# Odd taps of S through ScalarE and GpSimd, and the order of a turn's side work, in a chain of modulated 1-D convolutions

## Chip, core and metric

The kernel runs on one core of one Trainium2 chip. The metric is device time in microseconds of one execution; the kernel before takes 475.72 us (median of three runs, 475.56 to 475.97). Engines are named as in the profile: PE is TensorE's matmul, PEld its weight load, DVE is VectorE, ACT is ScalarE, POOL is GpSimd, SP is SyncE, which issues nearly all DMAs.

## The reference

x is (128, 64, 1024), the style (128, 128). Four layers of a convolution of 3 taps, 64 to 64 channels, whose weights are scaled per sample by the style and normalised, follow each other without a nonlinearity; the second doubles the length and blurs, the fourth blurs and halves it. The result is added to x.

```python
def _layer(x, style, w, b, mw, mb, typ):
    s = style @ mw.T + mb
    weight = SCALE * w * s[:, None, :, None]
    demod = lax.rsqrt(jnp.sum(weight * weight, axis=(2, 3)) + EPS)
    weight = weight * demod[:, :, None, None]
    if typ == 'same':
        out = jax.vmap(_conv_same)(x, weight) + b[None, :, None]
    elif typ == 'upsample':
        out = jax.vmap(_conv_up)(x, weight.transpose(0, 2, 1, 3)) + b[None, :, None]
        out = _blur(out, 2.0 * blur_k, (1, 1))
    elif typ == 'downsample':
        xb = _blur(x, blur_k, (2, 2))
        out = jax.vmap(_conv_down)(xb, weight) + b[None, :, None]
    return out
...
out = x
for i, typ in enumerate(('same', 'upsample', 'same', 'downsample')):
    out = _layer(out, style, weights[i], biases[i], mod_w[i], mod_b[i], typ)
x = x + out
```

## The kernel before

All four layers are linear, so the kernel first multiplies their weights together: for each sample one convolution of 9 taps with 64 x 64 weights (Wf), and this is applied to x. The first and last three columns of each row, where padding matters, are computed on their own ("ends"), in pieces spread over the run.

Work is grouped in 32 groups q of four samples. Matmuls use the array as four quarters of 64 x 64, so one group's four samples go through it together; each fp32 matmul leaves two records in the trace. The stages of a group, with the tiles that they write:

- scale3 (ACT): wd, the scaled taps of the last layer. For q of 3 and more the tile holds five blocks: three taps and two sums of neighbours (w3x).
- stage1 (PE, ACT): psS is the product of wd with the weights of the layer before, S its five scaled taps. For q of 0, 1, 2 and 6 this is done directly by stage1. For the others stage1_a and stage1_b use a scheme with seven products instead of nine: stage1_a forms four of the blocks from five products, copied with the factor tBn (the negative of tB); stage1_b adds two more products into PSUM, from which two taps come by a VectorE instruction per half (L481: sum times tB minus a block), and GpSimd adds two blocks for one tap (L484).
- stage2 (PE, ACT): psR is S times the blurred up-sampling taps E, R its seven scaled taps. From group 8 to 30 sums of S are shared: share_sums (DVE) writes two more slots of S, share (PE) multiplies them into an unused stretch of the bank of psA, share_copy (ACT) copies the result into psR as seeds, and stage2_rest adds the rest.
- stage3_b, stage3_a (PE, ACT): psA and psW, then Wf. r_sums (POOL) makes two sums of R for the last products of stage3_b; four ACT copies seed psW for stage3_a.
- combine_a, combine_b (DVE): H, three sums of taps for a convolution with five products where nine would be needed.
- in_g01, in_g2 (DVE), in1, in2 (POOL), in3, in04 (DVE): the matching sums G and T of three planes of x. X is loaded plane by plane into two buffers.
- conv3, conv1, conv2 accumulate in psA, conv4 in Y, conv0 in psA; copy_m3 (ACT), sum1 and sum2 (DVE) take the partial results out in between; outputs (ACT) writes the three output planes o, stored by SP.

The order on each engine is the order of the program text. A turn of the main loop (turn_of(q), groups 4 to 28) works on several groups at once: the convolution of q and of n = q + 1, stage 2 and 3 of c = q + 2, stage 1 of s = q + 4. On PE a turn reads: stage2_rest, conv2, stage3_b, conv4, stage3_a, conv3, stage1_a, conv0, stage1_b, share, conv1. The first four groups go through early_turn, which has the same pieces in another order: there S of group q + 3 is used by stage 2 at the start of the next turn, while in turn_of it is used two turns later. psS, psR and psW share one pair of PSUM banks. SIDE, TABLES and LATE are tables of small pieces (scale tables, ends) by turn: side(SIDE, q) runs VectorE pieces of up to a few instructions.

Of the kernel before, what the change touches and what calls it, by code (L numbers as in the profile page):

```python
# [54 lines left out]
C = 64  # L55
K = 3
# [7 lines left out]
def kernel(  # L64
# [381 lines left out]
    def stage1(q, pool=None, engs=(nc_a, nc_a), between=None):  # L446

        wd = chain[q]
        ps = unit(pool or ps_w, f"psS{q}")
        for k, (at, at1) in enumerate(((0, 3), (3, 1), (1, 4))):  # L450
            tap_matmul(ps, wd, at, 2, woi[2][:, k, :], EVEN, first=k == 0)
            tap_matmul(ps, wd, at1, 1, woi[2][:, k, :], slice(1, 2), last=k == K - 1)
        if between:
            between()
        st, _ = s_tiles(q)
        for r in range(2):
            scaled_copy(engs[r], flat(st[r][:, 1:6]), ps[r][:, : 5 * C], tB[:, q, r : r + 1])
        chain[q] = st
        return ps

    def stage1_a(q, ps=None):

        ps = ps or unit(ps_w, f"psS{q}")
        wd = chain[q]
        tap_matmul(ps, wd, 2, 2, w2n[:, 0, :], EVEN, first=True)
        tap_matmul(ps, wd, 3, 2, w2n[:, 2, :], EVEN)
        tap_matmul(ps, wd, 1, 1, w2n[:, 1, :], slice(1, 2))
        st, t = s_tiles(q)
        for r in range(2):
            scaled_copy(nc_a, flat(st[r][:, :4]), ps[r][:, C : 5 * C], tBn[:, q, r : r + 1])  # L470
        chain[q] = wd, ps, st, t

    def stage1_b(q):

        wd, ps, st, t = chain[q]
        tap_matmul(ps, wd, 2, 1, w2n[:, 3, :], slice(3, 4))
        tap_matmul(ps, wd, 4, 1, w2n[:, 4, :], slice(4, 5), last=True)
        for r in range(2):
            p1 = st[r][:, 0:1, :].to_broadcast([P, 2, C])
            sums = ps[r][:, 2 * C : 6 * C].rearrange("c (a b o) -> c a b o", a=2, b=2)[:, :, 0]  # L480
            nc_v.scalar_tensor_tensor(  # L481
                st[r][:, 4:6, :], sums, tB[:, q, r : r + 1], p1, op0=ALU.mult, op1=ALU.subtract
            )
        nc_g.tensor_add(t[:, :, 2], t[:, :, 2], t[:, :, 0])  # L484
        chain[q] = st
        whole[q] = t

# [10 lines left out]

    def share_sums(q):
        t = whole[q]  # L500
        nc_v.tensor_add(t[:, :, 6:8], t[:, :, 1:5:3], t[:, :, 2:6:3])

    def chain_matmul(dst, weight, st, slots, last=False):
        for r, rows in enumerate(HALF):
# [10 lines left out]
    def share(q, ps):  # L515

        at = [NB + 4 + i * C for i in range(3)]
        p12, p34 = ([b[:, i:j] for b in ps] for i, j in zip(at, at[1:]))
        chain_matmul(p12, E[:, 2], chain[q], slice(6, 7))
        chain_matmul(p34, E[:, 6], chain[q], slice(6, 7))  # L520
        chain_matmul(p34, E[:, 5], chain[q], slice(7, 8), True)
        shared_ps[q] = [b[:, at[0] : at[2]] for b in ps]

    def share_copy(q):
# [10 lines left out]
    def stage2_rest(q):  # L535

        ps = shared_ps.pop(q)
        block = lambda i, n=1: [b[:, i * C : (i + n) * C] for b in ps]
        apart = [b[:, : 4 * C].rearrange("c (a b o) -> c a b o", a=2, b=2)[:, :, 0] for b in ps]
        plan = (  # L540
            (apart, E[:, 0], slice(1, 4, 2)),
            (block(1), Ed[:, 0], slice(2, 3)),
            (block(2), Ed[:, 1], slice(1, 2)),
            (block(3), E[:, 2], slice(3, 4)),
            (block(3), Ed[:, 2], slice(2, 3)),
            (block(4), Ed[:, 3], slice(1, 2)),
            (block(4), E[:, 4], slice(3, 4)),
            (block(5, 2), E[:, 8], slice(2, 4)),
            (block(5), E[:, 6], slice(3, 4)),
            (block(1, 2), E[:, 1], slice(4, 6)),  # L550
            (block(2), E[:, 3], slice(4, 5)),
            (block(3), Ed[:, 4], slice(5, 6)),
            (block(4), Ed[:, 5], slice(4, 5)),
            (block(5), E[:, 7], slice(5, 6)),
        )
# [21 lines left out]
    def stage2_taps(q, taps, ps):  # L577

        st = chain[q]
        for n in taps:  # L580
            e = n - 2
            if e % 2 == 0:
                a, lo, m = slice(1, 4), e // 2 + 1, 3
            else:
                a, lo, m = slice(4, 6), (e + 3) // 2, 2
# [1136 lines left out]
```

## Time and profile before

| | us |
|---|---|
| median of three runs | 475.72 |
| span of the profiled execution | 475.5 |
| PE, convolutions on psA (L803, T with H) busy | 185.9 |
| PE, convolutions on psA and Y (L803, T with Wf) busy | 63.7 + 62.4 |
| PE, stage 2 with sharing (L506, psR) busy | 46.8 |
| DVE, G in two pieces (L712) busy | 49.0 + 27.7 |
| DVE, odd taps of S (L481) busy, 56 instructions | 16.7 |
| ACT, S from psS in stage1_a (L399) busy, 56 instructions | 23.5 |
| POOL, addition in S (L484) busy, 28 instructions | 21.6 |

For the profiled execution there is no time but its span; the three runs beside it were timed by themselves. In a profile row of the order of time the first number is the start in us from the span's start, the second the length, then engine, line, operation, the tiles as out<-in, and the count; in brackets stands idle time of the engine just before, with what ended it. "issue" is a stop for which the trace shows no semaphore. The granted TensorE clock is 0.998 of full speed on average. DMA moves 149 GB/s on average: 70.71 MB, nearly all on queue q1.

### The profile page before, as it was taken

The page shows a single profiled execution, that of the slowest core. Times are in us where ns is not written, and L with a number is a line of the kernel's source. Part 1 is how long each engine was busy: PE and PEld are TensorE (multiplying, and loading weights), DVE is VectorE, ACT ScalarE, POOL GpSimd, SP SyncE. Part 2 cuts the span into 40 slices and gives each one's busy share as a digit, 9 for nine tenths or more (in the row PEclk, how much of TensorE's full clock was granted, in tenths as well). Part 3 has the DMA queues.
Part 4 walks back from the last instruction along what each step waited for, and adds up shares of the span by engine and source line. Part 5 has one row for each costly group of instructions (what it writes and reads, how often), then busy time and mean ns, then how long its engine had stood idle before and what let it go on. Part 6 is the DMA issues. An engine that isn't in the chain of part 4 may idle for free.

```text
span 475.5 us, 26771 instructions
## 1 busy us (share of the span) xinstructions
PE 469.7 (99%) x11932; PEld 349.5 (74%) x11932; DVE 417.3 (88%) x694; ACT 312.0 (66%) x711; POOL 165.8 (35%) x200
## 2 busy tenths in 40 slices
PE   9999999999999999999999999999999999999996
PEld 6987788777678876677776677766788787876653
DVE  3889998879989998899979899979998999999896
ACT  4565657577766676766667666667666777766464
POOL 3634033664444342233432233422333423243200
PEclk9999999999999999999999999999999999999999
DMA  5237456535445554345544454543555544455225
GB/s 176 71 115 224 150 151 180 152 113 177 139 145 166 166 166 136 123 150 169 163 150 126 130 168 152 178 124 121 152 164 169 164 145 147 148 152 161 80 91 193
DMA packets 52707, 70.71 MB, mean 149 GB/s; under 512 B 6000, under 2 KB 50672, under 8 KB 52592
## 3 DMA queue, kind: packets, MB, share of 16 engines
q1 hardware_dynamic: 52368, 68.78, 46.3%
q8 instruction: 93, 1.52, 1.4%
q10 hardware_dynamic: 224, 0.22, 0.1%
q14 instruction: 22, 0.18, 0.1%
HBM read 35.36 MB, written 33.62 MB: 145 GB/s over the span
## 4 chain that ended last, share of the span: by engine, by line
PE 99%; DVE 0%; ACT 0%; issue 0%
PE psA L803 47%; PE Y L803 12%; PE psR L506 9%; PE psW L621 7%; PE psA L621 7%; PE psS L428 6%; PE psR L589 5%; PE psA L506 2%; PE Y L1044 2%; PE Y L183 1%; PE Y L379 1%; PE psM L220 0%; PE psE L1044 0%; PE Y L255 0%; DVE o L882 0%; PE psM L255 0%
## 5 line engine op out<-in xcount | busy, mean ns | idle before, releaser
L803 PE MATMUL psA<-T,H 64*64 64x340 f32 x2304 | 185.9, 446 | 0.0
L803 PEld LDWEIGHTS psA<-T,H 64*64 64x64 f32 x2304 | 90.7, 133 | 46.9 <-issue 2.5
L712 DVE SCALAR_TENSOR_TENSOR G<-X 128x1376 f32<-128x1376 f32 (+2 forms) x65 | 78.0, 1206 | 0.2
L776 POOL TENSOR_TENSOR T<-G 128x684 f32<-128x684 f32 x28 | 46.3, 1652 | 73.7 <-DVE G L712 73.7
L484 POOL TENSOR_TENSOR S<-S 128x128 f32<-128x128 f32 x28 | 21.6, 772 | 139.7 <-ACT S L399 139.6
L399 ACT ACTIVATE R<-psR,tC 128x448 f32<-128x448 f32 x63 | 36.6, 631 | 43.6 <-PE psR L506 25.8
L803 PE MATMUL psA<-T,Wf 64*64 64x340 f32 x768 | 63.7, 446 | 0.0
L803 PE MATMUL Y<-T,Wf 64*64 64x340 f32 x768 | 62.4, 451 | 0.0
L712 DVE SCALAR_TENSOR_TENSOR Y<-m,psA 128x340 f32<-128x340 f32 x62 | 32.0, 516 | 28.2 <-PE psA L803 26.9
L399 ACT ACTIVATE psW<-psA 128x128 f32<-128x128 f32 x100 | 19.3, 268 | 49.1 <-PE psA L621 45.0
L790 DVE TENSOR_TENSOR T<-G 128x1368 f32<-128x1368 f32 (+1 forms) x33 | 50.8, 1541 | 0.0
L399 ACT ACTIVATE Wf<-psW,t 128x256 f32<-128x256 f32 (+2 forms) x76 | 32.7, 480 | 26.7 <-PE psW L621 26.4
L761 DVE TENSOR_TENSOR T<-X 128x684 f32<-128x684 f32 x32 | 47.7, 1492 | 0.0
L506 PE MATMUL psR<-S,E 64*64 64x64 f32 (+1 forms) x1472 | 46.8, 237 | 0.0
L781 POOL TENSOR_TENSOR T<-G 128x684 f32<-128x684 f32 x28 | 46.5, 1660 | 0.0
L428 PEld LDWEIGHTS psS<-wd,w2n 64*64 64x64 f32 x1120 | 35.1, 133 | 12.9 <-issue 0.3
L506 PEld LDWEIGHTS psR<-S,E 64*64 64x64 f32 x1472 | 39.5, 134 | 4.9 <-ACT psR L529 0.2
L803 PEld LDWEIGHTS Y<-T,Wf 64*64 64x64 f32 x768 | 30.3, 132 | 16.8
L803 PEld LDWEIGHTS psA<-T,Wf 64*64 64x64 f32 x768 | 29.8, 133 | 14.5
L880 ACT ACTIVATE o<-psA,tb,td 128x340 f32<-128x340 f32 x63 | 37.1, 648 | 5.0 <-PE psA L803 2.8
L880 ACT ACTIVATE o<-y,tb,td 128x340 f32<-128x340 f32 x62 | 38.5, 678 | 0.0
L880 ACT ACTIVATE o<-Y,tb,td 128x340 f32<-128x340 f32 x62 | 36.1, 639 | 2.8 <-PE Y L803 2.0
(180 smaller groups left out, 840.4 us busy)
## 6 DMA issues: line engine op xcount, KB each, us to landing
out<-o SPq DMA_DIRECT2D x191, 170.0 KB, 2.6
X<-in_x SPq DMA_DIRECT2D x150, 172.0 KB, 3.4
X<-in_x SPq DMA_DIRECT2D x14, 516.0 KB, 5.0
par<-in_params SPq DMA_DIRECT2D x3, 192.0 KB, 3.8
Xe<-in_x_ends SPq DMA_DIRECT2D x1, 512.0 KB, 4.5
out<-Oe SPq DMA_DIRECT2D x2, 96.0 KB, 2.1
out<-o ACTq DMA_DIRECT2D x1, 170.0 KB, 2.8
par<-in_params SPq DMA_DIRECT2D x1, 160.0 KB, 2.7
```

Source lines behind the costliest of these rows:

```text
L399: nc_a.activation(dst, src, AF.Copy, scale=f)
L428: nc.tensor.matmul(ps[r][cols, at * C : (at + n) * C], weight[rows], wd[c if r == 0 else 1 - c][rows, taps], start=first, stop=last, skip_ ...
L506: nc.tensor.matmul(dst[r][cols], weight[rows], st[c if r == 0 else 1 - c][rows, slots, :], start=False, stop=last, skip_group_check=True,)
L589: nc.tensor.matmul(ps[r][cols, lo * C : (lo + m) * C], E[rows, e + 2, :], src[rows, a, :], start=(n == 0), stop=(n == 8), skip_group_check ...
L621: nc.tensor.matmul(dst[r][cols], weight[rows], t[rows, c, slots, :], start=first, stop=last, skip_group_check=True,)
L712: nc_v.scalar_tensor_tensor(out, x, f, y, op0=ALU.mult, op1=op)
L761: nc_v.tensor_sub(t[:, pairs, 0, :NJ], plane(X, 3, pairs), plane(X, 1, pairs))
L776: eng.tensor_add(t[:, :, 0, :NJ], plane(g, 2), plane(g, 1))
L781: eng.tensor_sub(t[:, :, 1, :NJ], plane(g, 2), plane(g, 1))
L790: nc_v.tensor_sub(t[:, pairs, :, :NJ], both(a, PL), both(b, 1))
L803: nc.tensor.matmul(ps[s][cols, :NB], w, Ts[q, tag][rows, c, i, g : g + NB], start=(g == 0 and (m == 3 or alone)), stop=(g == K - 1), skip_ ...
L880: nc_a.activation(dst, src, AF.Identity, bias=add, scale=d3)
```

## The change

S's five taps take slots 0 to 4 in their own order (before: 1, 4, 2, 5, 3), and all readers follow. stage1 multiplies each tap in one matmul of three blocks instead of one of two and one of one. stage1_a copies its four blocks into slots 0, 2, 4 and 6, and GpSimd's addition comes there. stage1_b copies the two odd sums by ScalarE into slots 1 and 3, and GpSimd subtracts the block in slot 6 from both; VectorE's instruction is gone. In turn_of, scale3(s) stands behind stage2's copies of R instead of at the end of the turn before; share and share_copy stand ahead of outputs(q, 1); in_g01 follows in_g2; the side pieces stand at the end of the turn before theirs, behind in3 and in1.

```diff
-        for k, (at, at1) in enumerate(((0, 3), (3, 1), (1, 4))):
-            tap_matmul(ps, wd, at, 2, woi[2][:, k, :], EVEN, first=k == 0)
-            tap_matmul(ps, wd, at1, 1, woi[2][:, k, :], slice(1, 2), last=k == K - 1)
+        for k in range(K):
+            tap_matmul(ps, wd, k, K, woi[2][:, k, :], slice(0, K), first=k == 0, last=k == K - 1)
...
-            scaled_copy(engs[r], flat(st[r][:, 1:6]), ps[r][:, : 5 * C], tB[:, q, r : r + 1])
+            scaled_copy(engs[r], flat(st[r][:, :5]), ps[r][:, : 5 * C], tB[:, q, r : r + 1])
...
     def stage1_a(q, ps=None):
-        tap_matmul(ps, wd, 2, 2, w2n[:, 0, :], EVEN, first=True)
-        tap_matmul(ps, wd, 3, 2, w2n[:, 2, :], EVEN)
-        tap_matmul(ps, wd, 1, 1, w2n[:, 1, :], slice(1, 2))
+        tap_matmul(ps, wd, 1, 2, w2n[:, 0, :], EVEN, first=True)
+        tap_matmul(ps, wd, 2, 2, w2n[:, 2, :], EVEN)
+        tap_matmul(ps, wd, 4, 1, w2n[:, 1, :], slice(1, 2))
         st, t = s_tiles(q)
         for r in range(2):
-            scaled_copy(nc_a, flat(st[r][:, :4]), ps[r][:, C : 5 * C], tBn[:, q, r : r + 1])
+            src = ps[r][:, C : 5 * C].rearrange("c (a o) -> c a o", o=C)
+            scaled_copy(nc_a, st[r][:, 0:7:2, :], src, tBn[:, q, r : r + 1])
+        nc_g.tensor_add(t[:, :, 2], t[:, :, 2], t[:, :, 6])
...
     def stage1_b(q):
-        tap_matmul(ps, wd, 2, 1, w2n[:, 3, :], slice(3, 4))
-        tap_matmul(ps, wd, 4, 1, w2n[:, 4, :], slice(4, 5), last=True)
+        tap_matmul(ps, wd, 1, 1, w2n[:, 3, :], slice(3, 4))
+        tap_matmul(ps, wd, 3, 1, w2n[:, 4, :], slice(4, 5), last=True)
         for r in range(2):
-            p1 = st[r][:, 0:1, :].to_broadcast([P, 2, C])
-            sums = ps[r][:, 2 * C : 6 * C].rearrange("c (a b o) -> c a b o", a=2, b=2)[:, :, 0]
-            nc_v.scalar_tensor_tensor(
-                st[r][:, 4:6, :], sums, tB[:, q, r : r + 1], p1, op0=ALU.mult, op1=ALU.subtract
-            )
-        nc_g.tensor_add(t[:, :, 2], t[:, :, 2], t[:, :, 0])
+            src = ps[r][:, C : 5 * C].rearrange("c (a b o) -> c a b o", a=2, b=2)[:, :, 0]
+            scaled_copy(nc_a, st[r][:, 1:4:2, :], src, tB[:, q, r : r + 1])
+        nc_g.tensor_sub(
+            t[:, :, 1:4:2], t[:, :, 1:4:2], t[:, :, 6:7].to_broadcast([P, 2, 2, C])
+        )
...
     def turn_of(q):
         stage2(c)
+        if s < NQ and not entry:
+            scale3(s)
...
         in_g2(c)
-        side(SIDE, q)
+        in_g01(c)
+        if entry:
+            side(SIDE, q)
+        conv0(q, *((2,) if entry else range(K)))
+        if entry:
+            conv1(n, 0, 1)
+        if s < NQ:
+            stage1_b(s)
         if q in SMALL:
             l, bs = SMALL[q]
             nc_v.memset(high(bs.stop - bs.start), 0.0)
-        conv0(q, *((2,) if entry else range(K)))
-        if entry:
-            conv1(n, 0, 1)
-        outputs(q, 1)
-        if s < NQ:
-            stage1_b(s)
-        in_g01(c)
         if sharing(q):
             share(c + 1, banks(q))
             share_copy(c + 1)
+        outputs(q, 1)
         outputs(q, 0)
...
         in1(c, nc_g)
-        if s + 1 < NQ:
-            scale3(s + 1)
+        side(SIDE, q + 1)
```

The readers of S (share_sums, share, stage2_rest, stage2_taps) change slot numbers only. Three places show what moves.

ScalarE in a turn of the main loop, from the copy m (of psA) on; y and psA are the sources of two output planes, psR the seeds, R the taps of stage 2, wd those of scale3. Before:

```order
L842 COPY m_13_3994<-psA_3884 128x680
L880 ACTIVATE o_3972<-y_12_3792,tb,td 128x340 x2
L529 COPY psR_0_4042<-psA_3614 128x256
L529 COPY psR_1_4043<-psA_3614 128x256
L880 ACTIVATE o_3972<-psA_3614,tb,td 128x340 x2
L399 ACTIVATE wd_0_4068<-w3x,tA 128x320
L399 ACTIVATE wd_1_4070<-w3x,tA 128x320
L399 ACTIVATE R_4128<-psR_0_4042,tC 128x448
L399 ACTIVATE R_4128<-psR_1_4043,tC 128x448
```

The same stretch of the change:

```order
L842 COPY m_13_3960<-psA_3849 128x680
L399 ACTIVATE S_3956<-psS_0_3942,tB 128x2x64
L399 ACTIVATE S_3956<-psS_1_3943,tB 128x2x64
L529 COPY psR_0_4003<-psA_3578 128x256
L529 COPY psR_1_4004<-psA_3578 128x256
L880 ACTIVATE o_3937<-y_12_3756,tb,td 128x340 x2
L880 ACTIVATE o_3937<-psA_3578,tb,td 128x340 x2
L399 ACTIVATE R_4091<-psR_0_4003,tC 128x448
L399 ACTIVATE R_4091<-psR_1_4004,tC 128x448
L399 ACTIVATE wd_0_4094<-w3x,tA 128x320
L399 ACTIVATE wd_1_4096<-w3x,tA 128x320
```

Two copies out of psS come in ahead of the seeds, the y outputs go behind the seeds, and the wd copies behind R.

VectorE in the same turn, from in04 (L790) to the step on Y of sum2; G is written by in_g2 (342 columns twice) and in_g01 (688 twice), L501 is share_sums, L761 in3, Ye and g side work. Before:

```order
L790 TENSOR_TENSOR T_13_3996<-G_3729 128x4x342
L501 TENSOR_TENSOR S_3721<-S_3721 128x2x128
L712 SCALAR_TENSOR_TENSOR G_3999<-X_105 128x2x342
L1066 TENSOR_TENSOR Ye_161<-Ye_161,c_156 128x64x6
L481 SCALAR_TENSOR_TENSOR S_3991<-psS_0_3977,tB,S_3991 128x128
L481 SCALAR_TENSOR_TENSOR S_3991<-psS_1_3978,tB,S_3991 128x128
L712 SCALAR_TENSOR_TENSOR G_3999<-X_105 128x2x688
L712 SCALAR_TENSOR_TENSOR y_13_4062<-psA_3884,m_13_3994 128x680
L761 TENSOR_TENSOR T_14_4064<-X_105 128x2x342
L712 SCALAR_TENSOR_TENSOR Y<-m_13_3994,psA_3884 128x340 x2
```

The same stretch of the change:

```order
L790 TENSOR_TENSOR T_13_3962<-G_3694 128x4x342
L501 TENSOR_TENSOR S_3685<-S_3685 128x2x128
L712 SCALAR_TENSOR_TENSOR G_3965<-X_105 128x2x342
L712 SCALAR_TENSOR_TENSOR G_3965<-X_105 128x2x688
L712 SCALAR_TENSOR_TENSOR y_13_4027<-psA_3849,m_13_3960 128x680
L761 TENSOR_TENSOR T_14_4029<-X_105 128x2x342
L1016 SCALAR_TENSOR_TENSOR g_159<-par,g_159 128x192 x2
L712 SCALAR_TENSOR_TENSOR Y<-m_13_3960,psA_3849 128x340 x2
```

The two instructions on S are gone, the two pieces of G follow each other, and the side work (now that of the next turn) stands right ahead of the step on Y.

TensorE in stage1 of group 1, one tap before (psS is the result, wd the moving operand):

```order
L428 MATMUL psS_371<-wd_0_309,par 64x128
L428 MATMUL psS_371<-wd_1_311,par 64x128 x2
L428 MATMUL psS_371<-wd_0_309,par 64x128
L428 MATMUL psS_371<-wd_0_309,par 64x64
L428 MATMUL psS_371<-wd_1_311,par 64x64 x2
L428 MATMUL psS_371<-wd_0_309,par 64x64
```

and of the change all three taps:

```order
L428 MATMUL psS_359<-wd_0_297,par 64x192
L428 MATMUL psS_359<-wd_1_299,par 64x192 x2
L428 MATMUL psS_359<-wd_0_297,par 64x192 x2
L428 MATMUL psS_359<-wd_1_299,par 64x192 x2
L428 MATMUL psS_359<-wd_0_297,par 64x192 x2
L428 MATMUL psS_359<-wd_1_299,par 64x192 x2
L428 MATMUL psS_359<-wd_0_297,par 64x192
```

Eight matmuls of a tap become four, twelve fewer for each of the four groups that stage1 serves.

More of the change, by code (lines that the diff above doesn't have):

```diff
@@ L518, in share @@
         p12, p34 = ([b[:, i:j] for b in ps] for i, j in zip(at, at[1:]))
-        chain_matmul(p12, E[:, 2], chain[q], slice(6, 7))
-        chain_matmul(p34, E[:, 6], chain[q], slice(6, 7))
-        chain_matmul(p34, E[:, 5], chain[q], slice(7, 8), True)
+        chain_matmul(p12, E[:, 2], chain[q], slice(5, 6))
+        chain_matmul(p34, E[:, 6], chain[q], slice(5, 6))
+        chain_matmul(p34, E[:, 5], chain[q], slice(6, 7), True)
         shared_ps[q] = [b[:, at[0] : at[2]] for b in ps]
@@ L540, in stage2_rest @@
         plan = (
-            (apart, E[:, 0], slice(1, 4, 2)),
+            (apart, E[:, 0], slice(0, 5, 4)),
             (block(1), Ed[:, 0], slice(2, 3)),
-            (block(2), Ed[:, 1], slice(1, 2)),
-            (block(3), E[:, 2], slice(3, 4)),
+            (block(2), Ed[:, 1], slice(0, 1)),
+            (block(3), E[:, 2], slice(4, 5)),
             (block(3), Ed[:, 2], slice(2, 3)),
[L546 to L554, printed above, removed]
+            (block(4), Ed[:, 3], slice(0, 1)),
+            (block(4), E[:, 4], slice(4, 5)),
+            (block(5, 2), E[:, 8], slice(2, 5, 2)),
+            (block(5), E[:, 6], slice(4, 5)),
+            (block(1, 2), E[:, 1], slice(1, 4, 2)),
+            (block(2), E[:, 3], slice(1, 2)),
+            (block(3), Ed[:, 4], slice(3, 4)),
+            (block(4), Ed[:, 5], slice(1, 2)),
+            (block(5), E[:, 7], slice(3, 4)),
         )
```

6 lines of the change are left out of this document (3 added, 3 removed).

## The prediction

> **What bounds the kernel now.** I read the page first: shares by engine, the chain of work that ended last, and the DMA queues.
>
> ```profile
> PE 469.7 (99%) x11932; PEld 349.5 (74%) x11932; DVE 417.3 (88%) x694; ACT 312.0 (66%) x711; POOL 165.8 (35%) x200
> ...
> PE 99%; DVE 0%; ACT 0%; issue 0%
> ...
> q8 instruction: 93, 1.52, 1.4%
> ```
>
> TensorE carries 99% of the chain. VectorE is 88% busy but never on it, so work taken from VectorE shortens nothing by itself; only time in which TensorE issues no matmul can be won. Busy time hides such gaps, since matmul ends are modelled and bridge them. So I next measured whole turns of the main loop, from one copy of m to the next, in the view of busy time by stretches (length, then the busy time of PE, PEld, DVE, ACT, POOL):
>
> ```profile
> 140.73:154.73 14.00, 14.00 (x392) 11.33 (x388) 12.79 (x21) 9.79 (x25) 6.25 (x6) 1.00 0.50 154
> 225.87:239.71 13.84, 13.84 (x392) 9.84 (x388) 13.51 (x23) 9.86 (x25) 4.98 (x4) 1.00 0.49 157
> 342.68:356.86 14.18, 13.98 (x391) 11.26 (x387) 13.21 (x20) 9.85 (x24) 4.82 (x4) 1.00 0.49 151
> 398.47:412.40 13.93, 13.93 (x391) 11.26 (x387) 12.94 (x20) 9.87 (x25) 4.81 (x4) 1.00 0.50 154
> ```
>
> All four do the same matmuls. The shortest is 13.84 us, although VectorE is busy for 13.51 of it; the others are 0.16, 0.34 and 0.09 longer with a less busy VectorE. What they lose is seen in the order of time at 350 us:
>
> ```profile
> 346.75 4.06 SPq L146 DMA_DIRECT2D X<-in_x  x6
> ...
> 350.28 0.40 PE L621 MATMUL psA<-R,w0s 64*64 64x64 f32 x13
> ...
> 350.87 0.27 PE L621 MATMUL psA<-R,w0s 64*64 64x64 f32 x2 [0.20 <-issue]
> 350.87 0.13 PEld L621 LDWEIGHTS psA<-R,w0s 64*64 64x64 f32 x1 [0.33 <-issue]
> ```
>
> TensorE and its weight loads stop in the middle of a run of equal matmuls, with no semaphore to wait for ("issue"). I take this for missing instructions. The 11,932 matmul and 11,932 weight-load records over 93 packets of queue q8 are 257 to a packet, and 1.52 MB over 93 is 16 KB, so q8 brings TensorE's program in blocks. A turn has 384 matmul and 384 weight-load records (the windows also count the few that overlap their edges), three blocks almost exactly, so a block edge falls at nearly the same place turn after turn. Here that is inside stage3_b, behind the densest stretch (stage2_rest), while the X loads issued from 346.75 keep the DMA engines busy.
>
> The Trainium skill (Runtime: NRT & Kernel Launch, Instruction fetch mechanics) states blocks of 16 KiB, 256 instructions, fetched over a DMA queue, which agrees with the 257 above; it also calls the crossing mostly hidden, which the 0.33 us gap contradicts here. By its "hidden", this term below would be zero.
>
> **The change part by part.** First one turn as it is now:
>
> ```profile
> 211.86 0.87 DVE L712 SCALAR_TENSOR_TENSOR G<-X 128x684 f32<-128x684 f32 x1
> 212.21 0.82 POOL L484 TENSOR_TENSOR S<-S 128x128 f32<-128x128 f32 x1 [5.16 <-ACT S L399]
> 212.63 1.25 ACT L880 ACTIVATE o<-y,tb,td 128x340 f32<-128x340 f32 x2
> 212.80 0.41 PE L428 MATMUL psS<-wd,w2n 64*64 64x64 f32 x16
> 213.38 0.60 DVE L481 SCALAR_TENSOR_TENSOR S<-psS,tB,S 128x128 f32<-128x128 f32 x2
> 213.38 1.90 PE L803 MATMUL psA<-T,H 64*64 64x340 f32 x24
> 213.80 0.63 ACT L529 COPY psR<-psA 128x256 f32<-128x256 f32 x2
> 213.90 1.58 DVE L712 SCALAR_TENSOR_TENSOR G<-X 128x1376 f32<-128x1376 f32 x1
> 214.34 1.18 ACT L880 ACTIVATE o<-psA,tb,td 128x340 f32<-128x340 f32 x2
> 215.10 0.40 PE L506 MATMUL psR<-S,E 64*64 64x128 f32 x8
> 215.31 0.41 PE L506 MATMUL psR<-S,wsq 64*64 64x64 f32 x16
> 215.39 1.03 ACT L399 ACTIVATE wd<-w3x,tA 128x320 f32<-128x320 f32 x2
> 215.55 0.30 PE L506 MATMUL psR<-S,E 64*64 64x64 f32 x8
> 215.64 1.65 POOL L776 TENSOR_TENSOR T<-G 128x684 f32<-128x684 f32 x1 [2.61 <-DVE G L712]
> 216.21 1.81 DVE L761 TENSOR_TENSOR T<-X 128x684 f32<-128x684 f32 x1
> 217.33 1.16 ACT L399 ACTIVATE R<-psR,tC 128x448 f32<-128x448 f32 x2 [0.91 <-POOL T L776]
> 218.56 0.72 POOL L638 TENSOR_TENSOR R<-R 128x256 f32<-128x256 f32 x1 [1.27 <-ACT R L399]
> 219.00 1.07 DVE L712 SCALAR_TENSOR_TENSOR Y<-m,psA 128x340 f32<-128x340 f32 x2 [0.98 <-PE psA L803]
> 220.39 0.77 ACT L399 ACTIVATE psW<-psA 128x128 f32<-128x128 f32 x4 [1.90 <-PE psA L621]
> ```
>
> *ScalarE's queue.* Two new copies of 128x128 leave PSUM each turn. Bounds: half of the 0.77 that four such copies take at 220.39, and the 0.63 of the two 128x256 seeds; I take 0.5, nearer the same size. stage1_b ends on TensorE at 212.80 + 0.41 = 213.21, so the copies run to 213.75, the seeds to 214.4, the y outputs to 215.6 and the psA outputs to 216.8. The seeds are needed at 215.10, as safe as now. The R copies start when their matmuls end, 217.33: 0.5 us to spare, where now the scale copies end at 216.42. The scale copies follow R, 218.5 to 219.5, in the 1.90 us that ScalarE waits before 220.39. Cost in a turn: nothing. Behind R stands stage3_b, so every tenth by which this chain ran past 217.33 would be paid in full.
>
> *VectorE and GpSimd.* VectorE loses 0.60 in a turn, hidden before and after: its step on Y at 219.00 waits for TensorE (0.98). GpSimd gains a subtraction of 128x256, which I price by the 0.72 of the same size at 218.56 (bounds 0.46, what the addition takes alone at 40.63 below, and 1.3, were it slowed like the addition in this turn). That slowing matters: the addition takes 0.82 here beside VectorE's G, and VectorE's T<-X takes 1.81 here, ending 0.73 after GpSimd's T<-G (217.29), though half as big as G at 213.90 with 1.58. These pairs take turns. With G whole, GpSimd's addition ends at 213.0, G runs to some 214.6, the subtraction to 215.2, T<-G to 216.8, T<-X to 217.6, and side work of up to a microsecond
>
> ```profile
> 226.48 1.00 DVE L1016 SCALAR_TENSOR_TENSOR g<-par,g 128x192 f32<-128x192 f32 x2
> ```
>
> to 218.6. GpSimd's r_sums is due at 218.56, VectorE's Y at 219.00: it fits, with little left. I take no cost, and keep the other end as a rival.
>
> The Trainium skill (SBUF — State Buffer, Who interferes with whom) says that a VectorE instruction with two SBUF inputs and a GpSimd instruction that reads SBUF exclude each other, the first to issue holding on; the 1.81 and the 0.82 agree. That is its argument against moving work to GpSimd beside G.
>
> *First turns.* There S is used at the start of the next turn, and TensorE waits for VectorE's late reading of psS:
>
> ```profile
> 40.63 0.46 POOL L484 TENSOR_TENSOR S<-S 128x128 f32<-128x128 f32 x1
> 41.56 1.93 PE L803 MATMUL psA<-T,H 64*64 64x340 f32 x24
> 42.87 0.60 DVE L481 SCALAR_TENSOR_TENSOR S<-psS,tB,S 128x128 f32<-128x128 f32 x2
> 43.35 2.91 PE L589 MATMUL psR<-S,E 64*64 64x192 f32 x72
> ...
> 56.05 1.93 PE L803 MATMUL psA<-T,H 64*64 64x340 f32 x24
> 57.33 0.60 DVE L481 SCALAR_TENSOR_TENSOR S<-psS,tB,S 128x128 f32<-128x128 f32 x2
> 57.82 2.72 PE L589 MATMUL psR<-S,E 64*64 64x192 f32 x70
> ...
> 100.79 0.53 DVE L481 SCALAR_TENSOR_TENSOR S<-psS,tB,S 128x128 f32<-128x128 f32 x2
> 101.21 2.71 PE L589 MATMUL psR<-S,E 64*64 64x192 f32 x70
> ```
>
> A convolution occupies TensorE for 215.10 - 213.38 = 1.72 us, so psR could start at 43.28 and 57.77; it starts 0.07 and 0.05 late, and the second half of VectorE's pair (to 43.47 and 57.93) holds the other bank some 0.1 more each time. stage1_b stands on TensorE ahead of the last of conv0 and of the convolution at 41.56, so ScalarE's copies can be done by 41.56 + 0.5 and GpSimd's subtraction by 42.8; likewise by 57.3 in the second turn. I take -0.3 for these two, and -0.1 for the turn at 101 us, where the pair ends at 101.32, behind the start of psR. If the subtraction took its upper bound behind a busy GpSimd, each of the first three turns could pay the difference of 0.6 instead.
>
> *Fewer matmuls.* stage1 is used for four q; taps of 128 and 64 columns become one of 192. That removes 48 matmuls, 96 records, and no column. Eight records of 128 columns take 215.31 - 215.10 = 0.21, sixteen of 64 take 0.24: 26 ns against 2 x 15 = 30. So at most 96 x 4 ns = 0.4 us, at least nothing; these times carry 10 ns, and I take -0.1.
>
> *Instructions.* 48 matmuls are 96 matmul and 96 weight-load records, three quarters of a block, so later block edges fall 192 instructions further on in a turn, for these turns at the start of stage2_rest instead of its middle. The X loads stand behind the psA stores, which the new ScalarE order makes 1.2 us later. Edge and loads part. The three long turns above hold 0.59 of excess over 13.84; bounds are none of it and, with the smaller excess of other turns, 0.9. I take -0.5.
>
> Sum: -0.1 -0.4 -0.5 = -1.0, and some 0.1 from seeds that no longer wait for VectorE: -1.1. The profiled span is 475.5, 0.2 under the median of 475.72; taken off the median this gives 474.6.
>
> **The rivals.** *Only the waits go.* The gaps at block edges stay or move to other turns: then -0.5 is left, 475.2. For it: the edges still pass TensorE's dense stretch, and four other turns will get the place they have now. Against: turns with another place show no gap at all (225.87).
>
> *GpSimd and VectorE lock each other out.* Place: from G to r_sums. If the subtraction takes 1.3 instead of 0.72, T<-X ends at 218.2, a microsecond of side work at 219.2; Y is then 0.2 late and r_sums 0.6, stage3_b's last taps and conv4 wait, and the next turn starts later on VectorE too. It decides from the point where T<-G ends after 217.0. Price: 0.2 us in each of some 20 turns with side work, 4 us: 479. For it: the 1.81 and 0.82. Against: r_sums of the same size takes 0.72 beside VectorE's Y.
>
> *The new link is late.* GpSimd's subtraction in the first three turns (0.6 each), or R copies delayed by 0.05 us in 23 turns: +1.2 to +1.8, 477. Against: the 0.5 us margin.
>
> *The odd copies do not relieve anything* is the second half of "only the waits go": if VectorE's reading of psS was not what held psR, that case ends at 475.6.
>
> **How the numbers follow.** About 0.2%, 0.95 us, is what a measurement of this kernel tells from no change. Forecast 474.6, chance 0.52, own range 473.9 to 475.0, since the terms' bounds run from -0.7 to -1.8. Only the waits go: 0.26, 475.0 to 475.8. Lock: 0.14, 477 to 480. Late link: 0.08, 476.5 to 478. Below 474.77 counts as faster: most of the forecast and little else, 0.48. Same: the rest of it and nearly all of the second case, 0.30. Slower: the last two, 0.22. The range for all runs from 473.9 to 477.5; it leaves out the upper part of the lock case and the lowest sums.
>
> **What would show it.** Turns at 140, 342 and 398 us of 13.84 to 13.9 and no gap by issue inside L621: the block term is right. psR at 43 and 58 us starting 1.72 after the convolution's start: the psS term. T<-X ending near 217.6 on this turn's scale and r_sums directly behind R: no lock. Turns of 14.0 and more with Y waiting for nothing from TensorE would show the lock; R copies starting behind an output without a gap would show ScalarE as the new bound. The prediction is wrong if block edges move into another collision, or if an engine's order has a wait that these rows do not show.

## The result, and the profile after

The changed kernel is slower: 479.73 us median of five runs (478.35 to 480.46) against 475.97 us of the kernel before in the same session (475.56 to 477.39). The ratio is 1.0067, 95% interval 1.0047 to 1.0087. A second set of six runs of the same changed kernel gave 478.79 us against 475.79, ratio 1.0057 (1.0036 to 1.0078). The profiled execution took 479.67 us, span 477.9.

From the page of the changed kernel: the shares by engine, the chain that ended last, the packets that bring TensorE's program, and GpSimd's new group.

```profile
PE 469.0 (98%) x11836; PEld 351.4 (74%) x11836; DVE 398.1 (83%) x638; ACT 327.8 (69%) x767; POOL 197.3 (41%) x228
...
PE 97%; issue 1%; ACT 1%; DVE 0%; ACTq 0%
...
q8 instruction: 93, 1.52, 1.5%
...
L482 POOL TENSOR_TENSOR S<-S 128x256 f32<-128x256 f32 x28 | 31.2, 1116 | 25.7 <-ACT S L399 25.7
```

VectorE has lost 19 us of work, as meant, and TensorE has 96 records fewer. But "issue" has grown to 1% of the chain. Where the time went is read from stretches between copies of m. In the view of busy time by stretches (length, then the busy time of PE, PEld, DVE, ACT, POOL) two ordinary turns stand first, then three long ones:

```profile
226.45:240.29 13.84, 13.84 (x392) 9.79 (x388) 11.81 (x19) 10.40 (x26) 5.89 (x5) 1.00 0.51 155
344.35:358.19 13.84, 13.84 (x392) 9.79 (x388) 11.87 (x18) 10.40 (x27) 5.92 (x5) 1.00 0.51 158
...
63.66:80.29 16.63, 15.37 (x335) 12.49 (x331) 14.10 (x25) 11.04 (x23) 7.09 (x9) 1.00 0.45 131
182.01:198.77 16.76, 16.09 (x416) 11.16 (x412) 12.44 (x21) 10.40 (x27) 6.11 (x5) 1.00 0.46 132
240.29:256.47 16.18, 15.83 (x416) 11.13 (x412) 12.20 (x23) 10.40 (x27) 5.90 (x5) 1.00 0.46 134
```

Ordinary turns take 13.84 us, exactly as before; VectorE's relief shows there as idle time and as nothing else. In the kernel before, the three long turns read:

```profile
65.75:80.95 15.20, 15.19 (x332) 12.48 (x326) 12.60 (x27) 10.48 (x21) 5.13 (x8) 1.00 0.53 155
182.41:198.18 15.77, 15.77 (x416) 10.71 (x412) 12.94 (x25) 9.86 (x24) 4.81 (x4) 1.00 0.45 137
239.71:255.28 15.57, 15.57 (x416) 10.91 (x412) 12.16 (x22) 9.79 (x25) 4.97 (x4) 1.00 0.44 138
```

In the changed kernel PE's busy time falls short of their lengths by 1.26, 0.67 and 0.35. In the order of time for the weight loads the holes are these:

```profile
74.80 0.96 PEld L621 LDWEIGHTS psW<-R,par 64*64 64x64 f32 x19
77.27 0.14 PEld L621 LDWEIGHTS psW<-R,par 64*64 64x64 f32 x3 [1.50 <-issue]
...
189.82 0.13 PEld L506 LDWEIGHTS psR<-S,E 64*64 64x64 f32 x1 [0.83 <-issue]
...
247.52 0.19 PEld L506 LDWEIGHTS psR<-S,E 64*64 64x64 f32 x2 [0.46 <-issue]
```

Each is a stop amid equal matmuls with nothing to wait for. For the first one the view of the DMA queues lists only data between 70.0 and 74.9 us, and in the tenth of a microsecond from 74.9 this packet, with which the stop ends 2.3 us later:

```profile
q8 instruction: 1, 0.02, 58.8%
```

The stop at 350.87 us in the kernel before ends in the same way, 2.3 us after a packet of q8 started (348.53), and so does a smaller one of the changed kernel, 2.2 us after the packet at 263.99:

```profile
266.23 0.13 PEld L621 LDWEIGHTS psA<-R,w0s 64*64 64x64 f32 x2 [0.27 <-issue]
```

All three stand at the same place in a block: counted over all records of TensorE in the trace, 193 are left over by 256. The stops at 189.82 and 247.52 do not fit. They leave 185 and 255, the last packet ahead of them had started some 5.3 us before their end (184.47 and 242.24), and the next one came only behind them. That these two are late blocks is not shown.

To compare kernels I use the starts of four copies of m, at which the same matmuls stand. A is the first copy (the start), B the way from there to the turn at 98 us (the first turns), C from there to the turn at 427 us (the main loop), D to the last copy. The executions that follow are one profile each; the medians stand beside them.

| kernel | A | B | C | D | B+C+D | median |
|---|---|---|---|---|---|---|
| before | 23.09 | 75.04 | 328.16 | 34.46 | 437.66 | 475.97 |
| after | 21.20 | 76.53 | 329.66 | 35.10 | 441.29 | 479.73 |

So the change cost 3.6 us here between first and last copy: 1.5 in the first turns, 1.5 in the main loop, and 0.6 behind it, which fell to 0.2 in the second profile of the same kernel and to nothing in all others of the changed order.

### The profile page after: what moved, and what is told of

Read it like the earlier page. It is cut to its first block, busy times and chain, and to the rows that moved or that the text cites. A ratio compares the mean times of both kernels' runs of the same rounds, so it can differ in the third digit from the quotient of the medians.

```text
span 477.9 us, 26576 instructions
## 1 busy us (share of the span) xinstructions
PE 469.0 (98%) x11836; PEld 351.4 (74%) x11836; DVE 398.1 (83%) x638; ACT 327.8 (69%) x767; POOL 197.3 (41%) x228
## 4 chain that ended last, share of the span: by engine, by line
PE 97%; issue 1%; ACT 1%; DVE 0%; ACTq 0%
PE psA L803 46%; PE Y L803 12%; PE psR L506 9%; PE psW L621 7%; PE psA L621 7%; PE psS L428 5%; PE psR L589 5%; PE psA L506 2%; PE Y L1044 2%; PE Y L183 1%; PE psM L220 0%; PE Y L379 0%; PE psE L1044 0%; ACT S L399 0%; ACT o L880 0%
## 5 line engine op out<-in xcount | busy, mean ns | idle before, releaser
L803 PEld LDWEIGHTS psA<-T,H 64*64 64x64 f32 x2304 | 93.4, 133 | 44.6 <-issue 2.9
L712 DVE SCALAR_TENSOR_TENSOR G<-X 128x1376 f32<-128x1376 f32 (+2 forms) x65 | 83.2, 1318 | 0.2
L790 DVE TENSOR_TENSOR T<-G 128x1368 f32<-128x1368 f32 (+1 forms) x33 | 50.8, 1540 | 0.0
L712 DVE SCALAR_TENSOR_TENSOR y<-psA,m 128x680 f32<-128x680 f32 x31 | 26.9, 866 | 23.2 <-PE psA L803 21.8
L482 POOL TENSOR_TENSOR S<-S 128x256 f32<-128x256 f32 x28 | 31.2, 1116 | 25.7 <-ACT S L399 25.7
L638 POOL TENSOR_TENSOR R<-R 128x256 f32<-128x256 f32 x24 | 17.5, 731 | 51.7 <-ACT R L399 51.6
```

The lines of the kernel that those rows point to most:

```text
L482: nc_g.tensor_sub(t[:, :, 1:4:2], t[:, :, 1:4:2], t[:, :, 6:7].to_broadcast([P, 2, 2, C]))
L712: nc_v.scalar_tensor_tensor(out, x, f, y, op0=ALU.mult, op1=op)
L790: nc_v.tensor_sub(t[:, pairs, :, :NJ], both(a, PL), both(b, 1))
L803: nc.tensor.matmul(ps[s][cols, :NB], w, Ts[q, tag][rows, c, i, g : g + NB], start=(g == 0 and (m == 3 or alone)), stop=(g == K - 1), skip_ ...
```

## The experiments

**Is it only the place of the block edges?** A matmul has four entries in TensorE's program (two matmul and two weight-load records), so 64 matmuls make one block of 256. The change takes out 48; 16 small ones more put the edges of the kernel before where the change has them, and 48 put the changed kernel's back.

```
     zeros_to_y(2, 256, False)
+    zeros_to_y(8, 32, False)      # 16 matmuls; 16 and 24 sets for 32 and 48
```

> The kernel before, with 16 small matmuls of zeros (32 columns each) added in the setup. They are 64 entries of TensorE's program, and 64 and the -192 of the change differ by one block of 256, so from the fifth turn on the block edges fall where the changed kernel has them, while every other engine keeps its order of before. Blocks theory (edges of TensorE's program meet late block transfers): slower than before by 1.5 to 4 us, 477.5 to 480, with stops by "issue" of over 0.4 us in other turns than before. Rival, orders theory (the new orders of ScalarE, VectorE and GpSimd cost the time): as before, 475.6 to 477.4. The 16 matmuls themselves cost at most 0.3 us.

> The changed kernel with the same 16 small matmuls in the setup: its block edges fall 64 entries further on. Blocks theory: another time than 479.7, by 1 us or more to either side, and the stops of 1.5, 0.9 and 0.5 us at 77, 190 and 248 us are gone or changed. Orders theory: 478.4 to 480.5 and the same stops.

> The changed kernel with 32 small matmuls in the setup: block edges half a block further on. Blocks theory: again another time, 475.5 to 481, with stops by "issue" at other places. Orders theory: 478.4 to 480.5 and the same stops.

> The changed kernel with 48 small matmuls in the setup, as many as the change takes out of stage1: from the fifth turn on the block edges fall where the kernel before has them, but the engines keep the changed order. Blocks theory: most of the loss is gone, 475.5 to 477.5, and the stops of 1.5, 0.9 and 0.5 us at 77, 190 and 248 us with it. Orders theory: 478.4 to 480.5.

| kernel | A | B | C | D | B+C+D | median |
|---|---|---|---|---|---|---|
| before + 16 | 23.67 | 74.58 | 328.24 | 34.45 | 437.27 | 476.43 |
| after + 16 | 22.59 | 76.03 | 329.13 | 34.45 | 439.61 | 479.35 |
| after + 32 | 24.39 | 76.01 | 328.06 | 34.46 | 438.53 | 478.73 |
| after + 48 | 24.81 | 76.04 | 329.33 | 34.46 | 439.83 | 480.71 |

The theory fell in this form. The kernel before did not become slower with the other edges (ratio 1.0007, 0.9993 to 1.0021), and the changed kernel did not recover with the old ones. But C does move with the edges, by 1.6 us between the places, and with 32 it is as short as before. The edges alone do not lengthen it either: with 16 more, the kernel before has the edges of the change, and its C is 328.24. B, on the other hand, is 1.0 to 1.5 us too long wherever the edges are: a second cause. The medians also carry the matmuls' own cost, which I had under-estimated: the timeline rows of the zero matmuls, before and with 16 more, differ by 0.8 us, not 0.3.

```profile
3.18 1.13 PE L183 MATMUL Y<-Z 64*64 64x256 f32 x8
```
```profile
3.18 1.93 PE L183 MATMUL Y<-Z 64*64 64x256 f32 x40
```

**The second cause.** With 32 small matmuls no block stop covers the first turns, and the timeline of that kernel shows GpSimd, VectorE's H step, and then TensorE's wait:

```profile
73.48 0.73 POOL L482 TENSOR_TENSOR S<-S 128x256 f32<-128x256 f32 x1 [2.12 <-ACT S L399]
74.17 1.65 POOL L776 TENSOR_TENSOR T<-G 128x684 f32<-128x684 f32 x1
75.78 1.64 POOL L781 TENSOR_TENSOR T<-G 128x684 f32<-128x684 f32 x1
76.15 1.68 DVE L712 SCALAR_TENSOR_TENSOR H<-Wf 128x384 f32<-128x384 f32 x1
...
87.81 0.86 DVE L712 SCALAR_TENSOR_TENSOR y<-psA,m 128x680 f32<-128x680 f32 x1
...
88.81 0.80 PE L803 MATMUL psA<-T,H 64*64 64x340 f32 x8 [1.27 <-DVE y L712]
```

GpSimd's products T<-G stand behind the subtraction, the subtraction behind ScalarE's odd copies, and those behind an output and two roots of the variance. So the first product starts 74.17 - 66.85 = 7.3 us behind the turn's copy of m. H then runs into the second one: it takes 1.68 us and ends (77.83) 0.41 behind the product (77.42). VectorE has no idle time from there to y, so y is late. In the kernel before the same rows read:

```profile
70.05 0.46 POOL L484 TENSOR_TENSOR S<-S 128x128 f32<-128x128 f32 x1 [7.63 <-ACT S L399]
70.46 1.66 POOL L776 TENSOR_TENSOR T<-G 128x684 f32<-128x684 f32 x1
72.07 1.65 POOL L781 TENSOR_TENSOR T<-G 128x684 f32<-128x684 f32 x1
75.28 0.55 DVE L712 SCALAR_TENSOR_TENSOR H<-Wf 128x384 f32<-128x384 f32 x1
```

There the products start 4.7 us behind the copy of m at 65.75 (with a stop of 0.25 us in the weight loads on the way), are over before H begins, and H takes 0.55.

Two kernels test this from both sides: one puts only the first turns' odd taps back on VectorE, the other only delays GpSimd in the kernel before. Two more ask whether the stops come again and whether they need data traffic.

```
# first turns as before, with the 32 small matmuls
-            stage1_b(s)
+            stage1_b(s, True)    # odd taps by VectorE's scalar_tensor_tensor, no tensor_sub
# kernel before, GpSimd delayed once
+        if q == 2: [nc_g.tensor_sub(raw[:, :n_later], raw[:, :n_later], raw[:, :n_later]) for _ in range(3)]
         if q:
             in1(c, nc_g)
# without stores (the changed kernel here, the kernel before further down)
     def store(q, s, planes=slice(0, K), queue=nc.sync):
+        if 5 <= q < 28: return
```

> The changed kernel with the 32 small matmuls, and with the odd taps of the first turns (up to the one that starts at 80 us) read out of PSUM by VectorE as before, so that GpSimd has no subtraction there; from the turn at 98 us on everything is as changed. Late-link theory (GpSimd waits behind ScalarE's odd copies, its products T<-G come 1.7 us late and lock VectorE out of its H step, VectorE's y is late at 87 us): the two turns from 63.7 to 97.7 us shrink from 33.6 to 32.0 to 32.6 us, the wait of 1.48 us for y is under 0.3, and the median falls from 478.7 to 477.2 to 477.7. Rival (the first turns lose to block edges alone): they stay at 33.3 to 34.1 and the median at 478.2 to 479.2.

> The kernel before, with three subtractions of 128x192 in an unused buffer put into GpSimd's queue once, in the third turn ahead of its products T<-G: GpSimd is some 1.5 us later there, and nothing else is changed. Late-link theory: the two turns from 65.8 to 98.1 us grow from 32.4 by 1.0 to 1.5 us, by a wait for VectorE's y near 87 us, median 476.8 to 477.4. Rival (GpSimd's lateness is hidden, the loss comes from somewhere else): no change, 475.6 to 476.2.

> The changed kernel without the stores of the outputs of the turns from the sixth to the 28th (these outputs are not written). Blocks theory (a block of TensorE's program comes late when its transfer starts behind data in the DMA engines): the stops by "issue" of 0.87, 0.54, 0.34 and 0.24 us at 190, 248, 266 and 280 us fall under 0.1, and the time from 98 us to the end shrinks by about 2 us, median 477.3 to 478.3. Rival (a block edge costs TensorE its time wherever the DMA engines are): the stops stay, 479 to 480.5.

> The changed kernel once more, for a second profiled execution. If the stops by "issue" belong to the program, the ones of 1.5, 0.87 and 0.54 us at 77, 190 and 248 us come again at the same matmuls within 0.3 us; if they are chance, they stand elsewhere and the median still lies between 478.3 and 480.5.

| kernel | A | B | C | D | B+C+D | median |
|---|---|---|---|---|---|---|
| VectorE's odd taps in first turns, + 32 | 24.72 | 74.59 | 327.91 | 34.46 | 436.96 | 477.31 |
| before, GpSimd delayed | 22.64 | 76.07 | 327.67 | 34.45 | 438.19 | 477.42 |
| after without stores | 20.89 | 76.49 | 327.54 | 34.46 | 438.49 | 478.57 |
| after again | 23.19 | 76.28 | 329.37 | 34.68 | 440.33 | 478.79 |

The late link is shown from both sides. Undone, it gives back 1.42 us of B and 1.4 of the median. Put into the kernel before, it costs 1.50 in the two turns from 65 us, which took 31.95 us with the 16 matmuls and 33.45 here, and 1.6 of the median. The delayed kernel's rows are those of the changed one, H locked out and all; my three subtractions took 2.96 us instead of the expected 1.5, which happens to be the delay that the change makes (7.3 against 4.4 us behind the copy of m in the kernel before with 16 matmuls):

```profile
69.64 2.96 POOL L1472 TENSOR_TENSOR raw<-raw 128x448 f32<-128x448 f32 x3
72.55 1.66 POOL L776 TENSOR_TENSOR T<-G 128x684 f32<-128x684 f32 x1
74.17 1.65 POOL L781 TENSOR_TENSOR T<-G 128x684 f32<-128x684 f32 x1
74.36 1.87 DVE L712 SCALAR_TENSOR_TENSOR H<-Wf 128x384 f32<-128x384 f32 x1
...
87.20 0.80 PE L803 MATMUL psA<-T,H 64*64 64x340 f32 x8 [1.42 <-DVE y L712]
```

With VectorE's odd taps in the first turns, H takes its 0.55 us again and TensorE's wait for y is gone:

```profile
76.47 0.55 DVE L718 SCALAR_TENSOR_TENSOR H<-Wf 128x384 f32<-128x384 f32 x1
...
87.79 0.80 PE L809 MATMUL psA<-T,H 64*64 64x340 f32 x8
```

Without stores the main loop loses its stops: C is 2.1 us shorter, and the turns at 182 and 240 us are back at 15.78 and 15.56. (B keeps its 76.5, since the first turns' stores stay.) The same stretch of weight loads then shows no wait where 0.83 us stood:

```profile
188.43 0.21 PEld L506 LDWEIGHTS psR<-S,E 64*64 64x64 f32 x8
188.55 1.36 PEld L803 LDWEIGHTS psA<-T,H 64*64 64x64 f32 x24
```

The median (478.57) stands 0.3 above what I expected, although C fell as forecast, and only 0.2 below that of the changed kernel in the same session (478.79). What the stores cost is thus shown in C of one profile, not in the medians. Run again, the changed kernel had its late stop in the first turns once more (79.01 us, 1.26), and those of the main loop in the same three places: 0.27 at 191.0, 0.54 at 249.0 and 0.46 at 267.9. So the places belong to the program, the sizes only roughly.

**Can the loss be avoided?** Next I moved the edges by cutting the setup's zero matmuls differently, and tried to repair the link in the change's own manner. In these four kernels columns 256 to 383 of Y are no longer set to zero in the setup, so what is added up there later isn't the reference's.

```
-    zeros_to_y(2, 384)
-    zeros_to_y(2, 96, False)
+    zeros_to_y(2, 256)
+    zeros_to_y(9, 32, False)
...
-    zeros_to_y(2, 256, False)
+    zeros_to_y(11, 32, False)
# v23_fill: stage1_b(s, q == 2) and, in the turn behind it, stage1_b(s, True)
# g2_fill: var_root behind stage1_b, in1(c, nc_g) ahead of tensor_sub where q == 2;
#          the entry turn's memset of Y ahead of in_g01(c)
```

> The changed kernel with the zero matmuls of the setup cut differently (4 of 256 columns and 40 of 32 in place of 12 of 96 to 384): 32 matmuls more, as in the run with 32, but without the 1.6 us that those cost at the start. The block edges are those of that run, the loss in the first turns stays. Link and blocks theories together: 0.9 to 1.5 us over the kernel before, 476.7 to 477.4; by blocks alone 475.5 to 476.2; by orders alone 478.4 to 480.5.

> The same, and in the turns at 64 and 80 us the odd taps are read by VectorE as before; the two turns ahead of them keep the change's copies and so its gain of 0.2 us at 51 us. Link theory: the two turns take 31.9 to 32.2 us, the rest as in the run with VectorE's odd taps in all first turns; from the first copy of m to the last 436.7 to 437.0 us against 437.7 of before, median 474.6 to 475.4, against before 0.998 to 1.000. Rival: as without VectorE's odd taps, 476.7 to 477.4.

> The changed kernel with the same fill, all odd taps on ScalarE and GpSimd as changed, but in the turn at 64 us ScalarE's two roots of the variance stand behind its odd copies and GpSimd's first product T<-G ahead of the subtraction; in the turn at 98 us VectorE's small memset of Y stands ahead of G. Link theory: GpSimd's second product ends before VectorE reaches H, H takes 0.5 to 0.9 us and not 1.7, the wait for y is under 0.5 us, the two turns take 32.0 to 32.6 us, and the wait of 0.38 us at 101 us is under 0.1; median 475.0 to 476.2. Rival (the subtraction by itself costs the time): the two turns stay at 33.3 to 34.1, 476.7 to 477.4.

> The kernel before with the same cut of the zero matmuls: its block edges fall half a block further on, its orders stay. Blocks theory: some stops go and others may come, 474.8 to 476.8, and its first turns keep 31.9 to 32.4 us; it tells whether the version above beats the kernel before by its orders or by the place of its block edges alone.

| kernel | A | B | C | D | B+C+D | median |
|---|---|---|---|---|---|---|
| after_fill | 23.80 | 76.01 | 328.44 | 34.46 | 438.91 | 479.00 |
| v23_fill | 23.31 | 74.60 | 327.96 | 34.46 | 437.02 | 476.76 |
| g2_fill | 24.16 | 74.97 | 330.04 | 34.46 | 439.47 | 479.34 |
| before_fill | 23.60 | 74.57 | 328.61 | 34.51 | 437.69 | 478.55 |

The fill missed its purpose. With it the kernel before has the same B+C+D as without (437.69 against 437.66) and a median 2.9 us higher, so the fill costs that outside of this stretch, and all four medians lie above what I expected. Among themselves they say the same as above: VectorE's odd taps in two turns take 1.4 us out of B, and 437.02 is, to 0.02, what I expected of that kernel's B+C+D. In the fourth, GpSimd's new order works without VectorE's help; its timeline has the second product over before H, and H at 0.55:

```profile
72.70 0.72 POOL L483 TENSOR_TENSOR S<-S 128x256 f32<-128x256 f32 x1
73.39 1.64 POOL L782 TENSOR_TENSOR T<-G 128x684 f32<-128x684 f32 x1
...
75.92 0.55 DVE L713 SCALAR_TENSOR_TENSOR H<-Wf 128x384 f32<-128x384 f32 x1
```

B falls by 1.0 of the 1.4 us (76.01 to 74.97). So the subtraction by itself is not what costs most, its place in GpSimd's queue is. My second repair in that kernel was a mistake. The memset of Y, put ahead of G, waits for ScalarE's output of Y and holds G with it; y is then late, and TensorE's weight loads wait 2.15 us at 106.8; this turn takes 16.90 us against 14.75 in after_fill, which is why C is 330.04:

```profile
101.74 0.14 DVE L1528 MEMSET Y<- 128x96 f32 x1 [2.58 <-ACT o L881]
101.79 1.57 DVE L713 SCALAR_TENSOR_TENSOR G<-X 128x1376 f32<-128x1376 f32 x1
```

**The pieces together.** The last four kernels keep the reference's zeros. Three have VectorE's odd taps in the turns at 64 and 80 us, with 0, 4 or 8 of stage1's 12 taps cut in two as before the change; this moves the edges and adds no column.

```
         for k in range(K):
+            if q * K + k < 8:
+                tap_matmul(ps, wd, k, 2, woi[2][:, k, :], slice(0, 2), first=k == 0)
+                tap_matmul(ps, wd, k + 2, 1, woi[2][:, k, :], slice(2, 3), last=k == K - 1)
+            else:
                 tap_matmul(ps, wd, k, K, woi[2][:, k, :], slice(0, K), first=k == 0, last=k == K - 1)
```

> The changed kernel, and in the turns at 64 and 80 us the odd taps are read by VectorE as before; no matmul added, so the block edges stand where the change put them and the start is that of the changed kernel. Both theories together: the two turns pay the block stop of 1.3 to 1.5 us at 77 us but not the wait for y behind it, 33.2 to 33.6 us against 33.8 to 34.1; the stops near 190, 248 and 266 us stay; median 477.6 to 479.0. By the late link alone (block edges cost nothing): 31.9 to 32.4 us for the two turns, 475 to 476.

> The same, with 4 of the 12 taps of stage1 in two matmuls each as before: 16 matmuls more, all ahead of the turn at 37 us, no column more, and the block edges 64 entries further on. Blocks theory: other stops than in the run without them, two turns of 31.9 to 32.4 or 33.2 to 33.6 us as the edge falls, 475.0 to 478.0. Orders alone: as without them.

> The same with 8 taps of stage1 in two matmuls each: the block edges of the run with 32 small matmuls, at no cost at the start. Both theories: two turns of 31.9 to 32.3 us, 327.8 to 328.1 from the turn at 98 us to that at 427 us, 436.8 to 437.1 us from the first copy of m to the last against 437.7 before; median 474.8 to 475.9, against before 0.998 to 1.000. Orders alone: 477.5 to 480.

> The kernel before without the stores of the outputs of the turns from the sixth to the 28th (these are not written). Blocks theory: its stops by "issue" at 141, 347, 361 and 403 us go, and from the turn at 98 us to the one at 426 us it takes 327.4 to 327.7 us, as the changed kernel without stores (327.54), so that the steady turns of the two kernels cost the same. If the change's orders had made the steady turns longer or shorter, the two would differ by more than 0.2.

| kernel | A | B | C | D | B+C+D | median |
|---|---|---|---|---|---|---|
| v23 | 22.13 | 74.60 | 330.26 | 34.46 | 439.32 | 476.93 |
| v23_s4 | 22.90 | 74.61 | 328.74 | 34.46 | 437.81 | 476.29 |
| v23_s8 | 21.33 | 74.60 | 327.93 | 34.46 | 436.99 | 475.67 |
| before without stores | 22.22 | 74.64 | 327.62 | 34.46 | 436.72 | 476.17 |

Among the first three the median falls with B+C+D: with the link undone and the edges at the best of these places the loss is gone, 475.67 against 475.81 us in the same session, ratio 0.9995 (0.9984 to 1.0006). That ties with the kernel before; no version beat it. Other time counts too: the profile of v23 comes from the slowest of its twelve executions (478.68), and the kernel before without stores has the shortest B+C+D and yet a median of 476.17. The two kernels without stores take 327.54 and 327.62 us for the main loop, so the steady turns of the two orders cost the same in sum, to 0.1 us. The ends of these stretches are the copies of m, the changed kernel first:

```profile
97.38 0.73 ACT L842 COPY m<-psA 128x680 f32<-128x680 f32 x1 [0.96 <-PE psA L803]
424.92 0.73 ACT L842 COPY m<-psA 128x680 f32<-128x680 f32 x1
```
```profile
96.86 0.72 ACT L842 COPY m<-psA 128x680 f32<-128x680 f32 x1 [0.95 <-PE psA L803]
424.48 0.72 ACT L842 COPY m<-psA 128x680 f32<-128x680 f32 x1
```

Two expectations of v23 missed. The median (476.93) lies below the 477.6 to 479.0 expected, and the stop at 77 us didn't come, although the kernel has as many matmuls as the changed one and so the edge at the same place. In the changed kernel the packet came in the tenth from 74.9 us, 11.2 to 11.3 us behind the copy; here the view of the DMA queues has it between 71.3 and 71.5, 6.7 to 6.9 behind it:

```profile
q8 instruction: 1, 0.02, 71.8%
```

With GpSimd and ScalarE on time the packet was too. The stop at 77 us thus came only together with the late link, in all three profiles of the changed order with these edges (1.50, 1.26 and 1.48 us), and it covers the wait for y: behind it, TensorE's rows show none. The kernel v23 has one profile only, and which transfer held that packet up isn't settled.

## Why the prediction was wrong, by its own steps

It said 474.6 us in 473.9 to 477.5; the measured 479.73 lies above, and the kernel became slower instead of faster. Two steps failed: the term for the block edges, and the first turns with their rival, the late link. By the medians the link weighs more. With it undone at the change's own edges (v23) 1.1 us of loss is left (476.93 against 475.81), where the change cost 3.0 and 3.8; with the edges moved as well (v23_s8), none.

*Instructions, -0.5: failed.* The reading that a stop is a block that comes late is borne out for the one that it quotes, at 350.87, and the three long turns (140, 342, 398 us) fell to 13.84 as forecast. The step "Edge and loads part" was wrong. It looked only at those three turns and took the new place for harmless. Time was lost elsewhere: the turns at 182, 240, 256 and 272 us, without a stop before, became longer by 0.98, 0.61, 0.28 and 0.25 us, so the main loop lost 1.5 instead of winning 0.5. What the runs show of the size is a spread: with the changed order C was 327.9 to 330.3 over the places tried, with the order before 327.7 to 328.6, with no stores 327.5 and 327.6. So in these profiles the loss in C came with the change's order, the place of the edges and the stores together; the loads alone could not give its sign. The new ScalarE order moves the psA stores too, but that this shift is the reason is not shown, and neither is how the stores stop TensorE at 190 and 248 us.

*First turns, -0.4, and their rival at 0.08, the new link is late: the rival came, in one turn, and by the lock.* I priced it at 0.6 in each of three turns, for the longer subtraction. It cost 1.4 in one: the subtraction depends on ScalarE, so everything behind it in GpSimd's queue came 2.6 us later in this turn (7.3 against 4.7), onto VectorE's H, from which VectorE works without a gap until TensorE waits for its y. I had counted the subtraction and not what is queued behind it. The Trainium skill (SBUF — State Buffer, Who interferes with whom) states that a VectorE instruction with two SBUF inputs contends with a GpSimd instruction that reads SBUF. The H step agrees, 1.68 us beside GpSimd's product against 0.55.

What was foreseen for the first turns was half right. The waits of psR at 43 and 58 us are gone, worth 0.03 and 0.17 us by the turns' lengths (14.38 to 14.35, 14.44 to 14.27) instead of 0.3. The turn at 98 us, where I took -0.1, lost 0.16 (14.59 to 14.75); in v23 it takes 14.49, so that loss is the link's as well.

*Lock in the ordinary turn, 0.14, priced 479: didn't come.* Its condition was T<-G ending after 217.0; in the turn that starts 0.59 us later than the quoted one, T<-G ends at 215.64 + 1.65 = 217.29, so 216.7 on its scale. GpSimd's subtraction took 1.15 us there, nearer my upper bound of 1.3 than the 0.72 I took, and was still hidden. That the time came out near 479 is a coincidence.

*ScalarE's queue and VectorE's relief, 0: right* in the steady turns. *Merged matmuls, -0.1*: not separable. *Seeds, 0.1*: not seen, since ordinary turns take 13.84 us before and after. The smallest sum of the stated bounds is -0.5, not the -0.7 from which the upper end of the forecast's own range was worked out. Had the two losses not come, the change would have been worth next to nothing: v23_s8, which keeps all of it but VectorE's reading in two turns and two thirds of the merged matmuls, ties with the kernel before.

## What to carry to other kernels

When work moves to another engine's queue, price what stands behind it there, in the turn with the least slack and not in the ordinary one: a dependency on a late producer delays the whole queue. Where one engine is fed almost without a gap, its instruction count or the stores beside it can by themselves move a microsecond or two (C of 328.06 to 329.66 over four counts here, 327.54 without stores); judge an edit by its steady turns, or at several counts, before believing half a per cent either way. And relief for an engine that the chain never passes shows up as idle time.

## What the runs showed of the hardware

The start differs from run to run. In the profile of the kernel before, TensorE ran at little more than half its rate until about 9 us, in the first one of the changed kernel until about 5, with a granted clock shown as 1.00 in both. The same 32 records, before first:

```profile
4.90 2.41 PE L379 MATMUL Y<-par,idb 64*64 64x192 f32 x32
```
```profile
5.00 1.32 PE L379 MATMUL Y<-par,idb 64*64 64x192 f32 x32
```

It is not the change: in the second profile of the changed kernel these records take 2.41 us too, and the first copy of m comes at 23.19 us instead of 21.20. Over all profiles it came between 20.9 and 24.8, the latest with matmuls added in the setup. So single spans can't be compared as they are. The executions of one kernel spread by some 3 us (476.81 to 480.20 with 32 matmuls added); how much of that is the start is not shown.
